# Softmax denominators by 32x32 turns on VectorE instead of products with ones, in a block of attention, MLP and Fourier layer

## The chip, the cores and the metric

The kernel runs on one core of one Trainium2 chip. The metric is the device time in microseconds, the median of several runs. The engines are TensorE (PE; PEld is its weight load), VectorE (DVE), ScalarE (ACT), GpSimd (POOL) and SyncE (SP), which issues nearly all DMAs.

## The reference, cut to what matters

Two layers work on a 48x48 image with 768 channels: 2304 tokens. The first is a transformer block: layer norm, attention with 12 heads of 64 channels and relative positions, projection, MLP. The second filters in the Fourier domain. The change lies in the attention's softmax and what follows it:

```python
attn = jnp.einsum('bqc,bkc->bqk', q * scale, k)
rel_h = jnp.einsum('bhwc,hkc->bhwk', r_q, Rh)
rel_w = jnp.einsum('bhwc,wkc->bhwk', r_q, Rw)
attn = (attn.reshape(B * nh, H, W, H, W) + rel_h[:, :, :, :, None] + rel_w[:, :, :, None, :]).reshape(B * nh, H * W, H * W)
attn = jax.nn.softmax(attn, axis=-1)
out = jnp.einsum('bqk,bkc->bqc', attn, v)
...
out = out @ proj_w + proj_b
x = shortcut + out
```

## The kernel before, in words

All arithmetic is in f32. The kernel has stages: queries, keys and values (to 434 us in the profile), attention (434 to 1452), projection, MLP, Fourier layer.

Attention goes over six pairs of heads (`pr`, 0 to 5; the two heads of a pair are `j` = 0, 1, on 64 partitions each) and, within a pair, over six chunks of `G` = 384 queries (`c`, 0 to 5): 36 chunks. For one chunk the keys are gone through in 18 tiles of 128 (`kt`). For each, `scores` makes transposed scores, keys on partitions and queries along the row, by `content` (L560) and `position` (L569), and ScalarE takes the exponential of both heads at once (L579) into `exps`. No maximum is subtracted. VectorE adds the exponentials up over key tiles: `pairs` (L665) takes two tiles at a time, eight additions in a chunk, the first of them when four tiles are there; `acc` (L669) is their sum, 128 partitions by 2 heads by 384 queries. What is still to be added is the sum over the partitions.

Then come the products with the values, `products` (L592), in six pieces of three key tiles. `between` returns what is put ahead of which piece (a table `work` by piece, 0 to 5): the denominators ahead of piece 5; in chunks 0 to 2 a `relative` for the chunk three further on ahead of piece 0; in chunks 3 and 4 the `columns` of the next pair ahead of pieces 0 to 2, and in chunk 4 a `relative` ahead of piece 3; in chunk 5 two `relative`; none of these in the last pair for chunks 3 to 5. A `relative` makes small products (L292) into the one `small` bank of PSUM, which ScalarE copies twice and VectorE subtracts (L238, `row_lo` and `col_parts`), and issues 24 transfers from SyncE into `terms`. `fetch` and `fetch_values` load the next pair's queries, keys and values from DRAM.

`denominators` (L603) multiplies `acc` by ones, so that every one of 64 rows has the sum of its head; ScalarE copies that to `rden` (L608) and accumulates `sums`. After the products, `finish` copies `op` out of PSUM (L617), adds the value bias times the denominator (L618), inverts the denominator on VectorE (L621), multiplies (L623, which also reorders the queries from blocks to rows), adds the inverse to `inverse` on GpSimd (L624), and stores to `oT` in DRAM (L625). `sums` and `inverse` are later tested for overflow; the test decides by a branch whether a slower general path runs.

Next, the projection reads `oT` by token tile (`og`, L692), and `residual` loads `x` (L685).

The order of PE and SyncE in attention is the order of the program (`manual_schedule`), and so is ScalarE's in the loop over the chunks. VectorE and GpSimd are ordered by a planner, as are instructions outside those scopes.

Of the kernel before, what the change touches and what calls it, by code (L numbers as in the profile page):

```python
# [19 lines left out]
P = 128  # L20
# [26 lines left out]
def block_then_afno(  # L47
# [53 lines left out]
    k_d = [dram.tile([P, T], F32, name=f"k_d{i}") for i in range(NC)]  # L101
    v_d = dram.tile([T, C], F32, name="v_d")
    oT = dram.tile([C, T], F32, name="oT")

    big1 = ctx.enter_context(tc.tile_pool(name="big1", bufs=1))
    main = big1.tile([P, NT * C], F32, name="main")
# [84 lines left out]

    with ExitStack() as flag_scope:
        flag_pool = flag_scope.enter_context(tc.tile_pool(name="flag", bufs=1))
        sums = flag_pool.tile([P, NC * (T // G)], F32, name="sums")
        inverse = flag_pool.tile([P, G], F32, name="inverse")
        nc.vector.memset(inverse, 0.0)


# [5 lines left out]
        with ExitStack() as att:  # L204
# [338 lines left out]
            with tc.manual_schedule(engines={mybir.EngineType.PE, mybir.EngineType.SP}):  # L543
                with ExitStack() as qkv:
                    queries_keys_values(qkv)

                psum = att.enter_context(tc.tile_pool(name="ps_att", bufs=1, space=PSUM))
                small_banks(psum, 1)
                kv_b = att.enter_context(tc.tile_pool(name="att_kv_b", bufs=1))
                o_pool = att.enter_context(tc.tile_pool(name="att_o", bufs=2))  # L550

                by_column = o_pool.tile([P, HW, HW], F32, name="by_column", bufs=1)
                kv = [None, kv_b]
                exps = main.rearrange("p (n j q) -> p n j q", n=NT, j=2)

                def content(pr, c, kt, sp, first):
                    qT, kT = heads[pr][:2]
                    for j in range(2):
                        at = slice(64 * j, 64 * j + 64)
                        nc.tensor.matmul(  # L560
                            sp[:, j, :G], kT[at, ts(kt, P)], qT[at, ts(c, G)],
                            start=first, stop=not first,
                        )

                def position(pr, c, kt, sp, first):
                    a, b = divmod(kt, 3)
                    for j in range(2):
                        at = slice(64 * j, 64 * j + 64)
                        nc.tensor.matmul(  # L569
                            sp[:, j, :G], select[at, a % 2], ready[pr, c][at, a // 2, b],  # L570
                            start=first, stop=not first,
                        )

                def scores(pr, c, kt, p):

                    sp = psum.tile([P, 2, 512], F32, name="sp", bufs=3)
                    for n, part in enumerate((content, position)):
                        part(pr, c, kt, sp, n == 0)
                    nc.scalar.activation(p, sp[:, :, :G], AF.Exp, scale=HD**-0.5)  # L579

                def in_columns(pr, i):

                    q = heads[pr][0].rearrange("p (c b h w) -> p b w c h", c=6, b=3, h=8)
                    nc.scalar.copy(
                        by_column[:, ts(i, 8)].rearrange("p w (c h) -> p w c h", c=6),
                        q[:, i // 2, ds(8 * (i % 2), 8)],
                    )

                def products(op, v, kts):
                    for kt in kts:  # L590
                        for j in range(2):
                            nc.tensor.matmul(  # L592
                                op[ts(j, 64)], v[:, kt, ts(j, 64)], exps[:, kt, j, :],
                                start=(kt == 0), stop=(kt == NT - 1),
                            )

                made = {}

                def denominators(pr, c, acc):

                    den = small_bank()
                    for j in range(2):
                        nc.tensor.matmul(  # L603
                            den[ts(j, 64)], ones[:, 0:64], acc[:, j, :], start=True, stop=True
                        )
                    at = pr * (T // G) + c
                    rden = o_pool.tile([P, G], F32, name="rden", bufs=1)
                    nc.scalar.activation(  # L608
                        rden, den, AF.Identity, accum_out=sums[:, at : at + 1]
                    )  # L610
                    made[pr, c] = rden

                def finish(pr, c, op):

                    rden = made.pop((pr, c))
                    ot = o_pool.tile([P, G], F32, name="ot")
                    nc.scalar.copy(ot, op)  # L617
                    nc.vector.scalar_tensor_tensor(  # L618
                        ot, rden, col(V_VB + pr), ot, ALU.mult, ALU.add
                    )  # L620
                    nc.vector.reciprocal(rden, rden)  # L621
                    o = o_pool.tile([P, G], F32, name="o")
                    nc.vector.tensor_tensor(by_rows(o), by_blocks(ot), by_blocks(rden), ALU.mult)  # L623
                    nc.gpsimd.tensor_tensor(inverse, inverse, rden, ALU.add)  # L624
                    nc.sync.dma_start(out=oT[ts(pr, P), ts(c, G)], in_=o)  # L625

                def between(pr, c, acc):

                    last = pr == NC - 1
                    work = {5: [partial(denominators, pr, c, acc)]}  # L630
                    if c < 3:
                        work[0] = [partial(relative, pr, c + 3)]
                    elif not last and c < 5:
                        for n in range(3):
                            work[n] = [partial(columns, pr + 1, 3 * (c - 3) + n)]
                        if c == 4:
                            work[3] = [partial(relative, pr + 1, 0)]
                    elif not last:
                        work[0] = [partial(relative, pr + 1, 1)]
                        work[2] = [partial(relative, pr + 1, 2)]  # L640
                    if not last and c in (2, 3):
                        for n in range(3):
                            i = 3 * (c - 2) + n
                            work.setdefault(n + (1, 3)[c - 2], []).append(
                                partial(in_columns, pr + 1, i)
                            )
                    return work

                with tc.manual_schedule(engines={mybir.EngineType.Activation}):
                    for pr in range(NC):  # L650
                        for c in range(T // G):
                            if c == 1 and pr < NC - 1:
                                fetch(pr + 1, kv[(pr + 1) % 2])
                            if c == 2 and pr < NC - 1:
                                fetch_values(pr + 1)
                            if c == 4 and pr == NC - 1:
                                nc.sync.dma_start(
                                    out=pw, in_=proj_w.rearrange("(c p) f -> p c f", p=P)
                                )
                            pairs = o_pool.tile([P, 2, 2, G], F32, name="pairs", bufs=1)  # L660
                            for kt in range(NT):
                                scores(pr, c, kt, exps[:, kt])
                                if kt > 2 and kt % 2:
                                    so_far = exps[:, ds(0, 2)] if kt == 3 else pairs
                                    nc.vector.tensor_tensor(  # L665
                                        pairs, so_far, exps[:, ds(kt - 1, 2)], ALU.add
                                    )
                            acc = o_pool.tile([P, 2, G], F32, name="acc")
                            nc.vector.tensor_tensor(acc, pairs[:, 0], pairs[:, 1], ALU.add)  # L669
                            op = psum.tile([P, G], F32, name="op")  # L670
                            work = between(pr, c, acc)
                            for i in range(6):
                                for what in work.get(i, ()):
                                    what()
                                products(op, heads[pr][2], range(3 * i, 3 * i + 3))
                            finish(pr, c, op)

        ln2 = flag_scope.enter_context(tc.tile_pool(name="ln2", bufs=4))
        for i in range(4):
# [847 lines left out]
```

## Time and profile before

| | |
|---|---|
| time, median of 3 runs | 2884.89 us (2884.84 to 2886.05) |
| profiled execution | 2886.02 us, span 2884.2 us |
| PE busy in the span | 2835.7 us (98%) |
| DVE / ACT / POOL busy in the span | 1759.2 / 937.1 / 618.4 us |
| attention, 434 to 1452 us: PE busy | 1017.42 of 1018 us |
| granted TensorE clock, mean | 0.996 |
| L603 in the trace | 144 records of 486 ns (4 in a chunk) |

A row of the timeline gives start and length in microseconds, engine, line, operation, what is written and read, the shape and the number of instructions merged. A bracket at the end gives the idle time before it and what ended it. Consecutive TensorE records overlap, so that the distance from start to start, and not the length of one, is what a product takes of the stage.

### The profile page before, as it was taken

How to read it: one execution, taken by the hardware profiler on the slowest of the kernel's cores; microseconds unless marked ns; L12 is line 12 of the kernel's file. 1: busy time of each engine (PE TensorE's matmuls, PEld its weight loads, DVE VectorE, ACT ScalarE, POOL GpSimd, SP SyncE). 2: the span in 40 equal slices, each digit the busy share in tenths (PEclk: the TensorE clock that was granted, in tenths of full speed). 3: DMA queues.
4: the chain of work that ended last, by engine and by line, in shares of the span. 5: the costliest groups of instructions: out<-in, count | busy, mean ns of one | idle time of the engine just before them, and what ended most of it. 6: DMA issues, size and time to landing. Idle time of an engine off the chain costs nothing. (4 is left out here: it accounts for less than half of the span.)

```text
span 2884.2 us, 41229 instructions
## 1 busy us (share of the span) xinstructions
PE 2835.7 (98%) x15949; PEld 1727.6 (60%) x15949; DVE 1759.2 (61%) x2412; ACT 937.1 (32%) x1538; POOL 618.4 (21%) x589
## 2 busy tenths in 40 slices
PE   8999999999999999999999999999999999999998
PEld 5555655656565555565555555555555555556887
DVE  5343236767676767676723666675666666666665
ACT  1011125757566666565600211122111211112332
POOL 2303010000000000000043322333322322322433
PEclk9999999999999999999999999999999999999999
DMA  4323276262552626445242111212111211113254
GB/s 150 134 96 107 100 163 126 41 129 59 90 122 48 140 37 124 82 68 89 62 165 77 50 56 54 66 59 75 64 66 45 98 55 56 54 56 115 64 157 143
DMA packets 216572, 255.59 MB, mean 89 GB/s; under 512 B 22220, under 2 KB 197036, under 8 KB 214832
## 3 DMA queue, kind: packets, MB, share of 16 engines
q1 hardware_dynamic: 213928, 251.03, 34.1%
q8 instruction: 128, 2.10, 0.3%
q10 hardware_dynamic: 2440, 1.84, 0.2%
q14 instruction: 76, 0.62, 0.1%
HBM read 136.88 MB, written 52.20 MB: 66 GB/s over the span
## 5 line engine op out<-in xcount | busy, mean ns | idle before, releaser
L579 ACT ACTIVATE main<-sp 128x768 f32<-128x768 f32 x648 | 516.7, 812 | 34.1 <-PE sp L569 19.5
L665 DVE TENSOR_TENSOR pairs<-pairs,main 128x1536 f32<-128x1536 f32 x252 | 443.0, 1758 | 27.1 <-DVE pairs L665 0.9
L569 PE MATMUL sp<-terms,select 64*128 64x384 f32 x1296 | 413.4, 630 | 0.0
L1060 DVE TENSOR_TENSOR main<-o,main 128x384 f32<-128x384 f32 x540 | 299.0, 556 | 40.6 <-PE o L1058 2.1
L998 PE MATMUL h<-shared,w 128*128 128x384 f32 x864 | 296.7, 486 | 0.8 <-issue 0.8
L560 PE MATMUL sp<-shared 64*128 64x384 f32 x1296 | 266.9, 488 | 2.2 <-DVE o L460 2.2
L560 PE MATMUL sp<-qT,kT 64*128 64x384 f32 x1296 | 264.1, 484 | 0.0
L624 POOL TENSOR_TENSOR inverse<-inverse,rden 128x384 f32<-128x384 f32 x36 | 49.0, 1360 | 977.3 <-DVE rden L621 977.3
L449 PE MATMUL m<-main 128*128 128x384 f32 x756 | 246.4, 488 | 3.0 <-DVE main L176 2.4
L998 PEld LDWEIGHTS h<-shared,w 128*128 128x128 f32 x864 | 164.1, 190 | 116.6 <-issue 3.2
L998 PE MATMUL h<-shared,w1s 128*128 128x384 f32 x648 | 226.6, 486 | 0.0
L592 PE MATMUL op<-main,shared 128*64 128x384 f32 x1296 | 218.7, 487 | 0.0
L1004 ACT ACTIVATE hT<-c,vec 128x384 f32<-128x384 f32 x108 | 66.4, 615 | 465.9 <-DVE c L1010 465.8
L592 PE MATMUL op<-main,v 128*64 128x384 f32 x1296 | 217.7, 487 | 0.0
L449 PEld LDWEIGHTS m<-main 128*128 128x128 f32 x756 | 143.0, 190 | 104.0 <-issue 4.6
L1010 DVE TENSOR_TENSOR c<-h,u 128x384 f32<-128x384 f32 x108 | 60.1, 557 | 212.4 <-PE h L998 212.4
L1058 PE MATMUL o<-w,hT 128*128 128x384 f32 x432 | 175.4, 488 | 3.3 <-DVE mv L122 2.0
L1058 PE MATMUL o<-w2s,hs 128*128 128x384 f32 x432 | 175.0, 487 | 2.3 <-DVE hs L159 2.3
L569 PEld LDWEIGHTS sp<-terms,select 64*128 64x128 f32 x1296 | 126.0, 187 | 83.7 <-issue 0.5
L998 PEld LDWEIGHTS h<-shared,w1s 128*128 128x128 f32 x648 | 123.1, 190 | 85.9
L618 DVE SCALAR_TENSOR_TENSOR ot<-rden,vec,ot 128x384 f32<-128x384 f32 x36 | 23.5, 654 | 241.0 <-ACT ot L617 241.0
L158 POOL TENSOR_TENSOR w1s<-w 128x384 f32<-128x384 f32 x36 | 36.7, 1020 | 604.7 <-PE o L1058 335.9
(161 smaller groups left out, 4079.0 us busy)
## 6 DMA issues: line engine op xcount, KB each, us to landing
w<-in_mlp_w_dram SPq DMA_DIRECT2D x72, 768.0 KB
terms<-col_parts SPq DMA_DIRECT2D x432, 72.0 KB
terms<-row_hi SPq DMA_DIRECT2D x216, 72.0 KB
terms<-row_lo SPq DMA_DIRECT2D x216, 72.0 KB
main<-in_qkv_w_dram SPq DMA_DIRECT2D x36, 384.0 KB
z<-zt SPq DMA_DIRECT2D x48, 192.0 KB
x<-in_x_blocks_dram SPq DMA_DIRECT2D x18, 384.0 KB
k_d<-o SPq DMA_DIRECT2D x36, 192.0 KB
```

Of the source, the lines that this page charges most:

```text
L449: nc.tensor.matmul(bank, a[:, c, :], b[:, c, :], start=(first and c == 0), stop=(c == 2), skip_group_check=not first,)
L560: nc.tensor.matmul(sp[:, j, :G], kT[at, ts(kt, P)], qT[at, ts(c, G)], start=first, stop=not first,)
L569: nc.tensor.matmul(sp[:, j, :G], select[at, a % 2], ready[pr, c][at, a // 2, b], start=first, stop=not first,)
L579: nc.scalar.activation(p, sp[:, :, :G], AF.Exp, scale=HD**-0.5)
L592: nc.tensor.matmul(op[ts(j, 64)], v[:, kt, ts(j, 64)], exps[:, kt, j, :], start=(kt == 0), stop=(kt == NT - 1),)
L624: nc.gpsimd.tensor_tensor(inverse, inverse, rden, ALU.add)
L665: nc.vector.tensor_tensor(pairs, so_far, exps[:, ds(kt - 1, 2)], ALU.add)
L998: nc.tensor.matmul(bank[i], a[:, c, :], b[:, c, :], start=(start and c == 0), stop=(c == 2), skip_group_check=not start,)
L1004: nc.scalar.activation(h[:, i, ts(k, G)], src, AF.Gelu, bias=col(V_B1 + 2 * n + i))
L1010: nc.vector.tensor_tensor(t, src, other, ALU.add)
L1058: nc.tensor.matmul(bank[k], a, b, start=start, stop=True, skip_group_check=not start)
L1060: nc.vector.tensor_tensor(dst, bank[k], dst, ALU.add)
```

## The change

The sum over partitions is made in another way. VectorE turns `acc` in blocks of 32x32 (`turned`), which puts 32 keys of a block along the row, and sums each 32 (`part`, 24 sums on each partition). One product of `part` with `gather` (a 128x32 matrix with a one where the partition is equal to the column modulo 32) adds the four groups of partitions; its result is 24 x 32, the 768 denominators of two heads by 384 queries, each once. `denominators` stands ahead of piece 1 and the product, in `inverses`, ahead of piece 4. VectorE inverts 24x32 values and adds to `sums`, and GpSimd adds to `inverse`.

To multiply the results, the inverses must stand on all 64 rows of their head. They are written to DRAM (`den_d`, `left_apart`) and read back with a broadcast (`spread_out`, two transfers), both from SyncE ahead of piece 5. A chunk's inverses are read back one chunk later than they are written, and used in `scaled` another chunk later. In the last pair from chunk 3 on they are read at once. `scaled` multiplies by `spread` on VectorE, and GpSimd then adds the value bias; `stored` stores the result a chunk later (in the last pair, from chunk 3 on, also at once). `finish` keeps only the copy out of PSUM. VectorE's order in the loop becomes that of the program, and `fetch_values` is called in chunk 3 in place of 2.

```diff
-        sums = flag_pool.tile([P, NC * (T // G)], F32, name="sums")
-        inverse = flag_pool.tile([P, G], F32, name="inverse")
+        sums = flag_pool.tile([P, 32], F32, name="sums")
+        inverse = flag_pool.tile([P, 32], F32, name="inverse")
...
+                ND = 2 * G // 32
+                gather = o_pool.tile([P, 32], F32, name="gather", bufs=1)
+                nc.vector.tensor_reduce(
+                    gather, ident.rearrange("p (g a) -> p a g", a=32), AX.X, ALU.add
+                )
+                parts = [o_pool.tile([P, 48], F32, name=f"part{i}", bufs=1) for i in range(2)]
...
                 def denominators(pr, c, acc):
 
+                    at = pr * (T // G) + c
+                    turned = o_pool.tile([P, 2 * G], F32, name="turned", bufs=1)
+                    nc.vector.transpose(turned, acc.rearrange("p j q -> p (j q)"))
+                    part = parts[at % 2]
+                    nc.vector.tensor_reduce(
+                        part[:, :ND], turned.rearrange("p (b i) -> p b i", i=32), AX.X, ALU.add
+                    )
+
+                def inverses(pr, c):
+
+                    at = pr * (T // G) + c
+                    part = parts[at % 2]
                     den = small_bank()
-                    for j in range(2):
-                        nc.tensor.matmul(
-                            den[ts(j, 64)], ones[:, 0:64], acc[:, j, :], start=True, stop=True
-                    at = pr * (T // G) + c
-                    rden = o_pool.tile([P, G], F32, name="rden", bufs=1)
-                    nc.scalar.activation(
-                        rden, den, AF.Identity, accum_out=sums[:, at : at + 1]
-                    )
+                    nc.tensor.matmul(den[:48, :32], part, gather, start=True, stop=True)
+                    rden = o_pool.tile([ND, 32], F32, name="rden")
+                    nc.vector.reciprocal(rden, den[:ND, :32])
+                    nc.vector.tensor_tensor(sums[:ND], sums[:ND], den[:ND, :32], ALU.add)
+                    nc.gpsimd.tensor_tensor(inverse[:ND], inverse[:ND], rden, ALU.add)
...
                 def finish(pr, c, op):
 
-                    rden = made.pop((pr, c))
-                    ot = o_pool.tile([P, G], F32, name="ot")
+                    ot = o_pool.tile([P, G], F32, name="ot", bufs=3)
                     nc.scalar.copy(ot, op)
-                    nc.vector.scalar_tensor_tensor(
-                        ot, rden, col(V_VB + pr), ot, ALU.mult, ALU.add
-                    )
-                    nc.vector.reciprocal(rden, rden)
-                    o = o_pool.tile([P, G], F32, name="o")
-                    nc.vector.tensor_tensor(by_rows(o), by_blocks(ot), by_blocks(rden), ALU.mult)
-                    nc.gpsimd.tensor_tensor(inverse, inverse, rden, ALU.add)
-                    nc.sync.dma_start(out=oT[ts(pr, P), ts(c, G)], in_=o)
+                    made[pr, c].append(ot)
+
+                def left_apart(pr, c):
+
+                    (rden,) = made[pr, c]
+                    nc.sync.dma_start(
+                        out=den_d[pr * (T // G) + c].rearrange("(n i) -> n i", i=32), in_=rden
+                    )
...
+                def spread_out(keep):
+
+                    while len(to_spread) > keep:
+                        pr, c = to_spread.pop(0)
+                        at = pr * (T // G) + c
+                        spread = o_pool.tile([P, G], F32, name="spread")
+                        for j in range(2):
+                            nc.sync.dma_start(
+                                out=spread[ts(j, 64)],
+                                in_=den_d[at, ts(j, G)].partition_broadcast(64),
+                            )
+                        to_scale.append((pr, c, spread))
+
+                def scaled(keep):
+
+                    while len(to_scale) > keep:
...
+                        nc.vector.tensor_tensor(
+                            by_rows(o), by_blocks(ot), by_blocks(spread), ALU.mult
                         )
+                        nc.gpsimd.tensor_scalar(o, o, col(V_VB + pr), None, ALU.add)
+                        results.append((pr, c, o))
...
                 def between(pr, c, acc):
 
                     last = pr == NC - 1
-                    work = {5: [partial(denominators, pr, c, acc)]}
+                    work = {
+                        1: [partial(denominators, pr, c, acc)],
+                        4: [partial(inverses, pr, c)],
+                        5: [partial(left_apart, pr, c), stored],
+                    }
+                    if last and c > 2:
+                        work[5] += [partial(spread_out, 0), partial(scaled, 1), stored]
+                    else:
+                        work[5] += [partial(spread_out, 1), partial(scaled, 1)]
...
-                with tc.manual_schedule(engines={mybir.EngineType.Activation}):
+                with tc.manual_schedule(
+                    engines={mybir.EngineType.Activation, mybir.EngineType.DVE}
+                ):
...
-                            if c == 2 and pr < NC - 1:
+                            if c == 3 and pr < NC - 1:
                                 fetch_values(pr + 1)
...
+                    scaled(0)
+                    stored()
```

More of the change, by code (lines that the diff above doesn't have):

```diff
@@ L103, in block_then_afno @@
     oT = dram.tile([C, T], F32, name="oT")
+    den_d = dram.tile([NC * (T // G), 2 * G], F32, name="den_d")
     big1 = ctx.enter_context(tc.tile_pool(name="big1", bufs=1))
@@ L193, in block_then_afno @@
         flag_pool = flag_scope.enter_context(tc.tile_pool(name="flag", bufs=1))
-        sums = flag_pool.tile([P, NC * (T // G)], F32, name="sums")
-        inverse = flag_pool.tile([P, G], F32, name="inverse")
+        sums = flag_pool.tile([P, 32], F32, name="sums")
+        inverse = flag_pool.tile([P, 32], F32, name="inverse")
+        nc.vector.memset(sums, 0.0)
         nc.vector.memset(inverse, 0.0)
@@ L595, in products @@
                             )
-                made = {}
-                def denominators(pr, c, acc):
-                    den = small_bank()
-                    for j in range(2):
-                        nc.tensor.matmul(
-                            den[ts(j, 64)], ones[:, 0:64], acc[:, j, :], start=True, stop=True
-                        )
-                    at = pr * (T // G) + c
-                    rden = o_pool.tile([P, G], F32, name="rden", bufs=1)
-                    nc.scalar.activation(
-                        rden, den, AF.Identity, accum_out=sums[:, at : at + 1]
-                    )
-                    made[pr, c] = rden
@@ L613, in finish @@
-                def finish(pr, c, op):
-                    rden = made.pop((pr, c))
-                    ot = o_pool.tile([P, G], F32, name="ot")
-                    nc.scalar.copy(ot, op)
-                    nc.vector.scalar_tensor_tensor(
-                        ot, rden, col(V_VB + pr), ot, ALU.mult, ALU.add
-                    )
-                    nc.vector.reciprocal(rden, rden)
-                    o = o_pool.tile([P, G], F32, name="o")
-                    nc.vector.tensor_tensor(by_rows(o), by_blocks(ot), by_blocks(rden), ALU.mult)
-                    nc.gpsimd.tensor_tensor(inverse, inverse, rden, ALU.add)
-                    nc.sync.dma_start(out=oT[ts(pr, P), ts(c, G)], in_=o)
+                ND = 2 * G // 32
@@ new lines, in block_then_afno @@
+                gather = o_pool.tile([P, 32], F32, name="gather", bufs=1)
[3 more added lines that the diff above has]
+                parts = [o_pool.tile([P, 48], F32, name=f"part{i}", bufs=1) for i in range(2)]
+                for part in parts:
+                    nc.vector.memset(part, 0.0)
+                def denominators(pr, c, acc):
+                    at = pr * (T // G) + c
[5 more added lines that the diff above has]
+                    )
@@ new lines, in inverses @@
+                def inverses(pr, c):
+                    at = pr * (T // G) + c
+                    part = parts[at % 2]
+                    den = small_bank()
+                    nc.tensor.matmul(den[:48, :32], part, gather, start=True, stop=True)
[3 more added lines that the diff above has]
+                    nc.gpsimd.tensor_tensor(inverse[:ND], inverse[:ND], rden, ALU.add)
+                    made[pr, c] = [rden]
@@ new lines, in block_then_afno, with finish @@
+                made, to_spread, to_scale, results = {}, [], [], []
+                def finish(pr, c, op):
+                    ot = o_pool.tile([P, G], F32, name="ot", bufs=3)
+                    nc.scalar.copy(ot, op)
+                    made[pr, c].append(ot)
[4 more added lines that the diff above has]
+                    )
+                    made[pr, c] = []
+                    to_spread.append((pr, c))
@@ new lines, in scaled @@
+                def scaled(keep):
+                    while len(to_scale) > keep:
+                        pr, c, spread = to_scale.pop(0)
+                        (ot,) = made.pop((pr, c))
+                        o = o_pool.tile([P, G], F32, name="o")
+                        nc.vector.tensor_tensor(
+                            by_rows(o), by_blocks(ot), by_blocks(spread), ALU.mult
+                        )
+                        nc.gpsimd.tensor_scalar(o, o, col(V_VB + pr), None, ALU.add)
+                        results.append((pr, c, o))
@@ L627, in between, with stored @@
+                def stored():
+                    while results:
+                        pr, c, o = results.pop(0)
+                        nc.sync.dma_start(out=oT[ts(pr, P), ts(c, G)], in_=o)
                 def between(pr, c, acc):
                     last = pr == NC - 1
-                    work = {5: [partial(denominators, pr, c, acc)]}
+                    work = {
[7 more added lines that the diff above has]
+                        work[5] += [partial(spread_out, 1), partial(scaled, 1)]
@@ L634, in between @@
                         for n in range(3):
-                            work[n] = [partial(columns, pr + 1, 3 * (c - 3) + n)]
+                            work.setdefault(n, []).append(partial(columns, pr + 1, 3 * (c - 3) + n))
                         if c == 4:
```

## The prediction

> **What bounds the kernel now.** I read the busy line of the page first, then the attention stage alone (the windows view), then one chunk in order of time, and last the rows of the lines that the change touches.
>
> ```profile
> PE 2835.7 (98%) x15949; PEld 1727.6 (60%) x15949; DVE 1759.2 (61%) x2412; ACT 937.1 (32%) x1538; POOL 618.4 (21%) x589
> ```
> ```profile
> 434.00:1452.00 1018.00, 1017.42 (x8537) 591.95 (x8536) 727.00 (x489) 627.96 (x895) 51.61 (x38) 1.00 0.46 90
> ```
>
> The second line has the window, its length, then busy time of PE, PEld, DVE, ACT and POOL, the granted clock, the DMA share and GB/s. In these 1018 us, which hold nearly all 36 chunks, PE is busy for 1017.42; VectorE has 291 us to spare, ScalarE 390, GpSimd nearly everything. So the stage ends when TensorE has done its instructions, and time is gained only by giving TensorE less or lost by making it wait. A busy PE may still be one whose records overlap, so the price of a product is read from starts, here one chunk's end on PE:
>
> ```profile
> 1008.79 0.93 PE L292 MATMUL small<-qT,relT 128*48 128x48 f32 x32
> 1009.55 9.86 PE L592 MATMUL op<-main,v 128*64 128x384 f32 x60
> 1019.24 0.81 PE L603 MATMUL small<-acc,ones 128*64 128x384 f32 x4
> 1019.88 2.10 PE L592 MATMUL op<-main,v 128*64 128x384 f32 x12
> 1021.92 0.92 PE L560 MATMUL sp<-qT,kT 64*128 64x384 f32 x4
> ```
>
> Column one is the start. The denominators (L603) start at 1019.24 and the next product at 1019.88: 0.64 us for four records, 0.16 each, though the source view gives 486 ns as the length of one (they overlap). A chunk with one `relative` takes 28.09 us (1021.91 less 993.82, the chunk starts).
>
> VectorE in the same chunk:
>
> ```profile
> 1013.96 0.96 DVE L669 TENSOR_TENSOR acc<-pairs 128x768 f32<-128x768 f32 x1
> 1014.83 0.55 DVE L238 TENSOR_TENSOR row_lo<-shared,row_hi 128x384 fp32r<-128x384 f32 x1
> 1022.55 0.62 DVE L618 SCALAR_TENSOR_TENSOR ot<-rden,vec,ot 128x384 f32<-128x384 f32 x1 [7.16 <-ACT ot L617]
> 1023.27 2.55 DVE L621 RECIPROCAL rden<-rden 128x384 f32<-128x384 f32 x1
> 1025.86 0.56 DVE L623 TENSOR_TENSOR o<-ot,rden 128x384 f32<-128x384 f32 x1
> 1026.41 2.48 DVE L665 TENSOR_TENSOR pairs<-main 128x1536 f32<-128x1536 f32 x1
> ```
>
> `acc` is ready at 1014.92, four microseconds ahead of its product: VectorE is off the path, by a margin that the change eats into.
>
> **What the Trainium skill says.** "VectorE: DVE Perf Modes", The three transpose paths: VectorE turns only 32x32 blocks, 128x128 bf16 in 311 ns. No turn is in this trace. The same page, Rules for kernel authors, says that a reduction runs at one element per cycle at best; the trace agrees: L719 with 36 elements took 191 ns, L720 with 384 took 553, 1.04 ns an element. "GPSIMD Engine Reference", Specifications: GpSimd shares SBUF interfaces with VectorE operations that have two SBUF inputs. The trace agrees: the first `pairs` addition takes 2.48 us beside GpSimd's `inverse` addition (1025.90 to 1027.27), and 1.76 in the first chunk, where GpSimd is idle. "DMA: Bandwidth & Descriptors", Anatomy of one DMA: some 2.0 us fixed for a transfer; the trace gives no landing times here, so I use it for the round trip through DRAM.
>
> **The change, part by part.** The sum is made against the profiled execution, 2886.02 us (span 2884.2), 1.1 over the median 2884.89; I take the difference off the median.
>
> 1. *Removed on TensorE*: 36 x 0.64 = **23.1 us**, all on the path.
> 2. *Added on TensorE*: one product of 48 columns of weights against 32 columns in two records (f32 gives two per product, as L603's four for two show). Nearest row: L292, 32 records of 48 columns from 1008.79 to 1009.55, 0.024 each, including the change to L592's shape. Two make 0.05; a 64-column weight load afterwards (137 ns) has no long product to hide under, so up to 0.2. I take 0.1: 36 x 0.1 = **3.6 us**. Bounds 1.8 and 7.2. Net 19.5.
> 3. *Turn and row sum on VectorE*, and its order fixed as written. The product now stands at piece 4, three k-tiles earlier: 12 records, 1.92 us. Its first weight load would come at 1018.92 (L603's) - 1.92 = 1017.00, or 3.04 us after `acc` starts. The first `pairs` addition loses its GpSimd neighbour and 0.72 us; the other seven follow at 1.85 us apiece (12.93 for seven), VectorE's own pace, so `acc` starts 0.72 earlier against the chunk: the limit is 3.76. It can't start earlier still, because the first addition already began at 1026.41, just when the fourth exponential was done (1023.07 + 4 x 0.82). From `acc`'s start: 0.87 to `row_lo`, 0.47 until the turn starts (the two follow at that distance elsewhere), turn 0.96, 0.09 between dependent operations, sum 0.95 (553 + 384 x 1.04). Sum **3.34**, 0.42 early. Cost zero, hidden under 12 products; without that cover it would be 1.9 us a chunk.
>  The turn is the unknown. Lower bound 0.96, one element per cycle as `acc` (128x768 in 958 ns). Upper: the skill's 311 ns scaled by six, an estimate of 1.87. I take 0.96, since 311 ns less the 0.16 fixed cost of these rows (958 - 768 x 1.04) leaves 1.2 ns an element, near the lower one. At 1.87 the product waits 0.5 us in the 18 chunks with c < 3, about 0.9 in the last pair's c = 3 to 5 (no `relative` ahead of the products there: `acc` to weight load is 2.33 + 0.72 = 3.05 against 3.05 used, no slack even now) and little elsewhere, since `columns` and a second `relative` add 0.76 us of PE each: 9 + 3 = 12 us. With the low value I charge 0.5 us for those last three.
> 4. *VectorE's other work*: gone are 0.62 + 2.55; new are a reciprocal of 32 (6.2 ns each by L621, some 0.35 us), an addition of 32 (0.19) and the moved product (0.56). With turn and sum the engine's 19.95 us in a chunk of 28.1 falls below 19. The small ones run from piece 4 on and end about 2 us before the chunk does; the next addition is due 4.5 us into the next chunk. Zero; VectorE isn't short of time.
> 5. *The new waits*. VectorE waits for `spread` ahead of the product `scaled`, with the next chunk's `pairs` behind it. `spread` was asked for one chunk before. SP is the queue that could make it late: each `relative` issues 24 transfers at 0.64 us, 15.4 us; from c = 4 to c = 0 of the next pair it issues without a pause. The change adds three transfers a chunk (one store, two reads), 2 us. There the reads of the fourth chunk leave some 25 us into chunk 0, just as VectorE wants them; with 2 to 4 us to land it idles until 28 or 29, and has until 28 + 4.5. Zero, with about 4 us of margin, five times in the kernel. `terms` are made two chunks ahead elsewhere; for c = 0 they are asked for a chunk ahead, before the new transfers. The moved `fetch_values` (1.15 MB) has over two chunks left. GpSimd's `inverse` addition shrinks and an addition of 128x384 (1.0 us) joins: idle otherwise.
> 6. *ScalarE* loses 0.49 + 0.19 us per chunk in a stretch in which it waits: zero.
> 7. *The end*. The last chunk's result goes through DRAM: two transfers of 2.0 us after the reciprocal, then 0.56 and 1.0. The reciprocal comes some 3 us before the products end, so the store leaves about 3 us after their end; before, it left at 1456.23, 6.3 after (1447.81 + 2.10). Loads for the projection (og, at 1437.5) stood ahead of that store; if they fall behind it TensorE waits up to 5 us, otherwise it neither gains nor loses. I take zero.
>
> Sum: -23.1 + 3.6 + 0.5 = **-19.0 us: 2886.0 becomes 2867.0, and the median 2866**. A measurement of this kernel can tell about 0.2% (5.8 us) from no change.
>
> **The rivals.**
> - *Part of the gain is waited away* (turn near 1.87 us, or the small product 0.2 us and the end 5 us): 12 us or 9 us back, 2874 to 2879. For it: the slack of 0.42 us is small, semaphores take part of it. Against: the skill's figure without its fixed cost. Chance 0.24.
> - *The small product waits for VectorE in nearly every chunk* and the kernel gets slower. Place: the weight load of `part` at piece 4, with six k-tiles of `products`, and then the next scores, behind it on PE. At 3.2 ns an element the turn takes 2.5 us: late by 1.1 in 18 chunks, 0.6 in five c = 5 chunks, 1.6 in three, 28 us, against 19.5 saved: 2893. It decides from a turn of about 2.1 us, where the waits eat the saving, and measures as slower from about 2.4. A `spread` that comes later than the 4 us of margin would add to it. Against: nothing on VectorE here but the reciprocal costs over 1.05 ns an element. Chance 0.13.
> - *Balanced*, between these: 2879.1 to 2890.7. Chance 0.07.
> - *The removed products were not on the path*, ScalarE being the bound with 18 x 0.82 us of exponentials: then no change. Against: it idles in the product pieces, and PE starts its first three score groups of a chunk, with free buffers, at the same 0.82 us. It is in the balanced case.
>
> **How the numbers follow.** The likeliest is the sum, 2866, chance 0.56. Faster: 0.56 + 0.24 = 0.80; within 0.2%: 0.07; slower: 0.13. The low end is the whole 23.1 saved with the small products nearly free, 2862 less a microsecond of noise; the high end takes in the partial rival and part of the balanced case: 2861 to 2882.
>
> **What would show it.** The `small` product with `part` and `gather` at about 0.1 us from start to next start, in place of 0.64; c = 1 chunks of 27.5 us in place of 28.09; the first `pairs` addition at 1.76 us; the turn as a row of about 0.96 us. Wrong would be: PEld waiting for the row sum in the list of waits, VectorE's `o` waiting for `spread` by more than 6 us, or a gap on PE between attention and projection.

## The result, and the profile after

| | before | after |
|---|---|---|
| time, median | 2885.47 us (2884.84 to 2887.24) | 2862.11 us (2861.51 to 2863.60) |
| profiled execution, its span | 2886.02, 2884.2 us | 2862.67, 2860.6 us |
| first score product to first projection product | 1033.3 us | 1013.5 us |

The ratio is 0.9919 (95% interval 0.9902 to 0.9936): faster by 23 us, 19 to 28. The first view is the page's busy line and the windows view of attention after (window, length, then busy PE, PEld, DVE, ACT, POOL, clock, DMA share, GB/s):

```profile
PE 2811.8 (98%) x15877; PEld 1733.5 (61%) x15877; DVE 1695.7 (59%) x2488; ACT 916.4 (32%) x1466; POOL 625.5 (22%) x625
```
```profile
434.00:1430.00 996.00, 995.42 (x8429) 596.15 (x8425) 666.69 (x564) 606.21 (x822) 58.70 (x71) 1.00 0.52 98
```

PE is as full as before, over a shorter stage: it still sets the end, and has less to do. The end of one chunk on PE, in order of time:

```profile
969.47 0.92 PE L294 MATMUL small<-qT,relT 128*48 128x48 f32 x32
970.23 7.93 PE L594 MATMUL op<-main,v 128*64 128x384 f32 x48
977.98 0.19 PE L623 MATMUL small<-gather,part 128*48 128x32 f32 x1
977.99 0.54 PE L594 MATMUL op<-main,v 128*64 128x384 f32 x1
978.01 0.21 PE L623 MATMUL small<-gather,part 128*48 128x32 f32 x1
978.06 4.06 PE L594 MATMUL op<-main,v 128*64 128x384 f32 x23
982.05 0.92 PE L562 MATMUL sp<-qT,kT 64*128 64x384 f32 x4
```

Products and small product together go from 970.23 to 982.05, 11.82 us; before, from 1009.55 to 1021.92, 12.37. The difference, 0.55, is what each chunk became shorter by: all 35 distances between one chunk's end and the next are 0.54 to 0.56 us less. VectorE in another chunk of the same kind:

```profile
986.54 1.76 DVE L725 TENSOR_TENSOR pairs<-main 128x1536 f32<-128x1536 f32 x1 [7.38 <-ACT main L581]
988.41 12.93 DVE L725 TENSOR_TENSOR pairs<-pairs,main 128x1536 f32<-128x1536 f32 x7
1001.37 0.96 DVE L729 TENSOR_TENSOR acc<-pairs 128x768 f32<-128x768 f32 x1
1002.25 0.55 DVE L240 TENSOR_TENSOR row_lo<-shared,row_hi 128x384 fp32r<-128x384 f32 x1
1002.72 0.97 DVE L612 STREAM_TRANSPOSE turned<-acc 128x768 f32<-128x768 f32 x1
1003.72 0.95 DVE L614 TENSOR_REDUCE part<-turned 128x24 f32<-128x768 f32 x1
1005.85 0.34 DVE L625 RECIPROCAL rden<-small 24x32 f32<-24x32 f32 x1 [1.17 <-PE small L623]
1006.12 0.12 DVE L626 TENSOR_TENSOR sums<-sums,small 24x32 f32<-24x32 f32 x1
1006.17 0.53 DVE L666 TENSOR_TENSOR o<-ot,spread 128x384 f32<-128x384 f32 x1
```

The turn takes 0.97 us. The row sum is there at 1004.67, and the small product's weight load starts 0.53 us later (the same in nearly every chunk with c < 3; 1.3 to 2.5 us with c = 3 to 5; 0.06 to 0.14 in the last three chunks). The bracket in the first row says that VectorE had stood idle for 7.38 us before this chunk's exponentials let it start: it is still off the path.

The stage is 19.8 us shorter, the medians differ by 23.4. The rest lies outside attention, where nothing was changed (us, one profiled execution each; e1 to e8 are the experiments below, e2 is code of before with one product cut):

| | up to the first score | projection | MLP | Fourier | sum |
|---|---|---|---|---|---|
| before | 417.2 | 151.4 | 1025.7 | 252.7 | 1847.0 |
| after | 416.4 | 150.0 | 1024.3 | 252.6 | 1843.4 |
| e2 | 416.8 | 151.3 | 1025.4 | 250.7 | 1844.2 |
| e6 | 416.7 | 150.3 | 1024.0 | 251.0 | 1842.0 |
| e8 | 418.7 | 151.2 | 1024.2 | 251.4 | 1845.5 |

In the traces of the ten kernels the sum goes from 1842.0 to 1847.0; the trace of before is the highest, and e2, with the same code outside attention, is 2.7 us below it. The kernel before itself took from 2878.72 to 2886.64 us in 23 runs on one chip. Most of the difference is granted clock, as the windows view shows in the projection, the first row before and the second after (the clock is the third number from the end):

```profile
1522.90:1529.70 6.80, 5.19 (x8) 2.83 (x9) 4.24 (x13) 0.88 (x3) 0.32 (x1) 0.50 0.59 188
1503.30:1506.70 3.40, 3.01 (x5) 1.82 (x6) 3.06 (x9) 0.59 (x2) 0.00 (x0) 0.50 0.52 148
```

TensorE ran at half clock for 6.8 us there before and for 3.4 us after. Over all ten traces, the seven with 6.8 us at half clock have a projection of 151.2 to 151.6 us, the three with 3.4 us one of 150.0 to 150.3. In the MLP the trace of before has two such stretches of 3.4 us and that of after one. At half clock 3.4 us hold 1.7 us of work, so that by estimate each further stretch costs up to 1.7 us; the two stages differ by 1.4 each. So 19.8 us belong to the change, and the other 3.6 to the executions that were traced.

### The profile page after: what moved, and what is told of

The parts are those of the page before. It is cut to its first block, busy times and chain, and to the rows that moved or that the text cites. A ratio compares the mean times of both kernels' runs of the same rounds, so it can differ in the third digit from the quotient of the medians.

```text
span 2860.6 us, 41333 instructions
## 1 busy us (share of the span) xinstructions
PE 2811.8 (98%) x15877; PEld 1733.5 (61%) x15877; DVE 1695.7 (59%) x2488; ACT 916.4 (32%) x1466; POOL 625.5 (22%) x625
## 5 line engine op out<-in xcount | busy, mean ns | idle before, releaser
L627 POOL TENSOR_TENSOR inverse<-inverse,rden 24x32 f32<-24x32 f32 x36 | 15.1, 418 | 959.7 <-DVE sums L626 916.2
L725 DVE TENSOR_TENSOR pairs<-main 128x1536 f32<-128x1536 f32 x36 | 63.3, 1759 | 250.6 <-ACT main L581 250.6
```

The lines of the kernel that those rows point to most:

```text
L725: nc.vector.tensor_tensor(pairs, so_far, exps[:, ds(kt - 1, 2)], ALU.add)
```

## Experiments

Ratios are to the kernel before in the same group of runs, with the 95% interval; its median was 2883.94 us in the group of e1 to e4 and 2886.91 in that of e5 to e8. "Attention" is from the first score to the first projection product, 1013.5 us in the changed kernel. All but e2 are edits of the changed kernel. In the traces of e1, e3 and e5 to e8 the first chunk is 0.8 us shorter for a reason that is not their edit: the others have half clock for 3.4 us at its start.

**e1: the products with ones put back.**

```diff
+                def with_ones(acc):
+                    den = small_bank()
+                    for j in range(2):
+                        nc.tensor.matmul(
+                            den[ts(j, 64)], ones[:, 0:64], acc[:, j, :], start=True, stop=True
+                        )
...
-                        5: [partial(left_apart, pr, c), stored],
+                        5: [partial(with_ones, acc), partial(left_apart, pr, c), stored],
```

> The changed kernel with the two products of acc with ones put back ahead of piece 5, their result unused: everything of the change stays but the removal on TensorE. If TensorE's time is the whole of the gain, it gives back 36 x 0.64 = 23 us and ends at 2885, within 2 us of the kernel before; each chunk longer by 0.64 us. If VectorE's shorter work or its fixed order brought part of the gain (rival), it stays below the kernel before by that part: at 2880 or less if that is 5 us. The stages before and after attention tell whether the 3.5 us that the two traces differ by outside of attention belong to the change (they stay at -0.8 and -2.7) or to the execution (they don't).

Measured: 2886.21 us, ratio 1.0010 (1.0003 to 1.0017); attention 1035.9, each chunk but the first 0.64 us longer than after and 0.09 longer than before. Everything else of the change together brings nothing. The 0.09 is the whole price of the small product, bare of what it replaces. Outside attention the differences that the expectation asks about come out at -0.4 and -2.9 us against the trace before, so they stayed; but e2, which has the code of before there, has -0.3 and -2.4. They belong to the trace of before and not to the change. The medians agree: over 20 and 23 runs they differ by 2.3 us, attention alone by 2.5.

**e2: the kernel before, with less product.**

```diff
-                            den[ts(j, 64)], ones[:, 0:64], acc[:, j, :], start=True, stop=True
+                            den[ts(j, 64), :32], ones[:, 0:64], acc[:, j, :32],
+                            start=True, stop=True,
...
-                    nc.vector.memset(bank, 0.0)
+                    nc.vector.memset(bank, 1.0)
```

> The kernel before with its products with ones cut to 32 of 384 columns, the rest of the denominators left out (what stands in the bank is taken in their place): TensorE's work taken away and nothing else of the change made. If TensorE's time is the whole of the gain: 36 x (0.64 - 0.15) = 18 us faster, 2867 to 2869, with VectorE's reciprocal of 2.55 us, the long first pairs addition of 2.48 us and ScalarE's copy all still there. If VectorE's relief was needed for the gain: 2875 or more.

Measured: 2864.74 us, ratio 0.9936 (0.9919 to 0.9952), 19.2 us less; attention 1014.2, 19.1 less than before. With the long reciprocal, the long first addition and ScalarE's copy all in place, nearly the same gain comes. e1 and e2 settle it from both sides: the gain is TensorE's time and not VectorE's.

**e3: each turn twice.**

```diff
+                    nc.vector.transpose(turned, acc.rearrange("p j q -> p (j q)"))
```

> The changed kernel with every turn done twice: the row sum is ready 1.0 us later. The trace after shows 0.53 us between the row sum's end and the weight load of the small product in the chunks with c < 3, 1.3 to 2.5 with c = 3 to 5, and 0.06 to 0.14 in the last three. If the small product waits on nothing else, PE then waits about 0.5 us (0.6 with the semaphore) in 18 chunks and 1.0 in the last three: 9 + 3 to 11 + 3 us, 2874 to 2876. If VectorE has other room that the trace doesn't show (rival): 2862 to 2866. If VectorE's order behind the turn holds up more than this product: 2880 or more.

Measured: 2870.09 us, ratio 0.9956 (0.9939 to 0.9972), attention 1020.7, 7.2 us more: 0.33 us in chunks with c < 3, none with c = 3 to 5, 0.64 in the last three. The place is as expected and the size is not. A waiting weight load starts 0.12 us after the row sum, so in c < 3 it was 1.01 - (0.53 - 0.12) = 0.60 late, and PE lost only 0.33. The rest is the weight load's lead, shown by the same chunk after (first row; its product starts at 977.98, above) and in e3:

```profile
977.66 0.12 PEld L623 LDWEIGHTS small<-gather,part 128*48 128x48 f32 x1 [0.18 <-issue]
```
```profile
981.91 0.16 PEld L624 LDWEIGHTS small<-gather,part 128*48 128x48 f32 x2 [0.79 <-issue]
981.94 0.20 PE L624 MATMUL small<-gather,part 128*48 128x32 f32 x1
```

After, the weights are loaded 0.32 us ahead of their product, while products of `op` still run; in e3 only 0.03 us ahead. So 0.29 us of lateness is absorbed.

**e4: the small product one piece earlier.**

```diff
-                        4: [partial(inverses, pr, c)],
+                        3: [partial(inverses, pr, c)],
...
-                            work[3] = [partial(relative, pr + 1, 0)]
+                            work[3].append(partial(relative, pr + 1, 0))
```

> The changed kernel with the small product ahead of piece 3 in place of 4 (in chunk 4 ahead of the relative there): 12 records of products, 1.92 us, of its cover are gone. From the margins in the trace after: 1.4 us of wait in 18 chunks, 0.2 in five with c = 3, about 0.2 in five with c = 4 (the relative now stands behind it), 0.6 in five with c = 5, 1.8 in three: 36 us, 2898, slower than the kernel before. If the wait is hidden by PE's own queue, or caught up by the scores (rival): 2862 to 2870.

Measured: 2902.87 us, ratio 1.0066 (1.0049 to 1.0083), attention 1051.9. Chunks lose 1.25 us with c < 3, 0.08 with c = 3, 0.46 with c = 5: each 0.12 to 0.15 less than expected, again by the lead of the weight load (in c < 3 it is 1.92 - 0.53 + 0.12 = 1.51 late, less 0.29). The last three lose 1.6 to 1.9, near the expected 1.8. Only c = 4 is far off, 1.58 against 0.2. The list of waits of e4 (who waited, for whom, us in total, times, longest), and one such chunk on PE:

```profile
PE small L623 <- DVE part L614: 24.4, 25, 1.7
PE small L294 <- DVE sums L626: 7.0, 5, 1.4
```
```profile
558.84 0.25 PE L623 MATMUL small<-gather,part 128*48 128x32 f32 x2
560.48 0.93 PE L294 MATMUL small<-qT,relT 128*48 128x48 f32 x32 [1.39 <-DVE sums L626]
```

The `relative` behind the small product writes the same PSUM bank, the only one of its kind, and waits until VectorE has read the denominators; on VectorE the two `col_parts` subtractions stand ahead of that. So the rival of the prediction that ends slower is a real one: three key tiles of cover, 1.92 us, are the difference between 0.8% faster and 0.7% slower.

**e5: written, read and used in one chunk.**

```diff
-                    if last and c > 2:
-                        work[5] += [partial(spread_out, 0), partial(scaled, 1), stored]
-                    else:
-                        work[5] += [partial(spread_out, 1), partial(scaled, 1)]
+                    work[5] += [partial(spread_out, 0)]
...
                             finish(pr, c, op)
-                    scaled(0)
+                            scaled(0)
```

> The changed kernel with the inverses read back and used in the same chunk: both reads stand behind the write ahead of piece 5, and the multiplication behind the copy of op, in every chunk. Only the distance between write, read and use is taken away. From the trace after: write to use took 7.7 us in the last chunk, where SP was nearly free. Where SP has no transfers of terms in hand (c = 3, and 4 and 5 of the last pair) VectorE gets spread some 3.5 us into the next chunk, in time for the additions due at 4.5: no loss. Where a relative has left 15 us of transfers in SP's queue, spread comes 11 us into the next chunk or later, VectorE stands still with the pairs behind it and the small product comes late by 7 us or more: over 18 chunks and more in the five with two relatives, 120 to 220 us, 2980 to 3080. If the waits on VectorE are absorbed by its 7.4 us of idle time per chunk (rival): 2862 to 2870, and the distance in pieces buys nothing.

Measured: 3181.50 us, ratio 1.1019 (1.1001 to 1.1037), attention 1335.9: worse than the worst expected. Waits of e5, VectorE's and PE's, then SP's queue:

```profile
DVE o L666 <- DMA spread<-den_d: 421.9, 23, 32.2
PE small L623 <- DVE part L614: 261.0, 28, 22.3
```
```profile
SPq L307 <- DVE row_lo L240: 217.6, 23, 15.4
SPq L641 <- DVE sums L626: 162.7, 8, 25.0
SPq L654 <- DMA den_d<-rden: 49.5, 36, 2.9
```

The waits close a loop: SP's transfers of `terms` from `row_lo` wait for VectorE, which stands still for `spread`, which SP issues only behind those `terms`. In one chunk, `row_lo` is made at 705.74, SP issues `terms` from 706.32 until the write of the inverses at 717.84 and the reads at 720.50, `o` starts at 724.00, the additions follow, and the next `row_lo` comes at 740.37: 34.6 us a turn, against 27.5 for PE's work. A chunk pays for the `relative` of the chunk before it. The 18 chunks behind one ahead of piece 0 lose 7.3 us on average, as expected. The five behind the one in c = 4, which stands ahead of piece 3, lose 14 to 16 us and were not counted, and the five behind two lose 24. Nor was the clock counted. A stretch of the same chunk behind its wait, in the windows view:

```profile
708.30:713.40 5.10, 5.09 (x18) 2.85 (x20) 0.39 (x2) 0.00 (x0) 0.24 (x1) 0.50 0.77 116
```

Around each of PE's 27 waits of 3.5 us and more, half the clock was granted, from 2.2 to 5.4 us into the wait to 2.8 to 5.9 us behind its end. PE waited for 262 us in all, and for 116 us more it worked at half clock, which by estimate costs 58: together 320 of the 322 us that were lost. A distance of one chunk opens the loop, as e8 shows, and is needed.

**e6: VectorE's order left to the planner.**

```diff
-                    engines={mybir.EngineType.Activation, mybir.EngineType.DVE}
+                    engines={mybir.EngineType.Activation}
```

> The changed kernel with VectorE's order left to the planner, as it was before, ScalarE's fixed. If the order as written is only a means of keeping the turn right behind acc and row_lo, and the planner puts them there too: 2862 within 2 us. If the planner puts the multiplication of an earlier chunk or other work ahead of the turn, or waits in another order, the small product is late by 0.5 us or more per chunk beyond its margin: 2870 or more (rival).

Measured: 2863.57 us, ratio 0.9924 (0.9907 to 0.9940), attention 1013.8. The planner sets the turn ahead of `row_lo`, and from the second pair on the margin with c < 3 is 0.87 us in place of 0.53. The chunks are as long as after but for the last, which is 1.1 us longer: the planner sets one `o`, which waits for `spread`, among its additions. That is all that the order written out brings.

**e7: GpSimd busy beside the first addition.**

```diff
+                    beside = o_pool.tile([P, G], F32, name="beside", bufs=1)
+                    for _ in range(6):
+                        nc.gpsimd.tensor_tensor(beside, ot, ot, ALU.add)
```

> The changed kernel with six additions of 128x384 with two inputs added on GpSimd at each chunk's start (their result unused), so that GpSimd works while VectorE makes the chunk's first pairs addition. If GpSimd's work beside it is what made that addition 2.48 us before and 1.76 after: it is again near 2.5 us or more here, the row sum comes at least 0.7 us later, and with a margin of 0.53 us, of which the weight load's lead gives 0.3 more, the small product is late by 0.1 us in 18 chunks and by 0.4 in three: 2 to 5 us, 2864 to 2867. If the length came from something else that the change removed (the operations before it on VectorE): 1.76 us still and 2862.

Measured: 2876.21 us, ratio 0.9964 (0.9952 to 0.9975), attention 1024.6. VectorE and GpSimd in one chunk of e7:

```profile
993.73 2.36 DVE L728 TENSOR_TENSOR pairs<-main 128x1536 f32<-128x1536 f32 x1 [7.38 <-ACT main L581]
996.19 13.57 DVE L728 TENSOR_TENSOR pairs<-pairs,main 128x1536 f32<-128x1536 f32 x7
```
```profile
990.03 6.75 POOL L639 TENSOR_TENSOR beside<-ot 128x384 f32<-128x384 f32 x6 [3.56 <-ACT ot L635]
996.75 2.74 POOL L672 TENSOR_SCALAR o<-o,vec 128x384 f32<-128x384 f32 x1
```

The first addition is long again, 2.36 us, beside GpSimd's additions. Its length does not follow the time spent side by side: here that is all of the addition, in the kernel before only the 0.86 us from 1026.41 to 1027.27, and it grew there by 0.72. The expectation counted only that one; the seven that follow took 13.57 in place of 12.93, beside GpSimd's one-input addition of the value bias, which was pushed there, and with c < 3 the row sum came 1.0 to 1.2 us late and not 0.7. With the 0.12 us of a waiting load, and less the margin of 0.53 and the lead of 0.29, that makes the 0.30 us (c = 0) and 0.54 (c = 1 and 2) that most of these chunks lost.

**e8: read back at once, used one chunk later.**

```diff
-                    if last and c > 2:
-                        work[5] += [partial(spread_out, 0), partial(scaled, 1), stored]
-                    else:
-                        work[5] += [partial(spread_out, 1), partial(scaled, 1)]
+                    work[5] += [partial(spread_out, 0), partial(scaled, 1)]
+                    if last and c > 2:
+                        work[5] += [stored]
```

> The changed kernel with the inverses read back in the chunk that wrote them in all chunks, and used one chunk later in place of two. SP now waits for the write to land, 3 to 4 us a chunk, ahead of the reads. If SP's room between two chunks' terms is enough (it issued without a pause from c = 4 to c = 0 of the next pair only, 60 us of 167): 2862 within 2 us, and VectorE's waits for spread at the pairs' borders (10 us in all, not paid by TensorE) shrink. If SP's waits push terms past the start of their chunk (rival), TensorE waits for terms at each pair's first chunks: 2870 or more.

Measured: 2864.16 us, ratio 0.9925 (0.9908 to 0.9942), attention 1012.7. SP waited 50 us in all for the writes, and nothing came late by it: behind the first, every chunk is as long as after, within 0.01 us. But VectorE's waits for `spread` did not shrink: 21.0 us in six, the one after the last chunk included, against 16.6 in seven after. One chunk of distance is enough, two buy nothing more. No version here beats the changed kernel by more than the spread of runs.

## Why the prediction was right

- *What bounds, and the removal (step 1).* Right: 0.64 us a chunk, by e1 and by the trace (36 of them are 23.0, not 23.1).
- *The small product (step 2).* Taken at 0.1, measured 0.64 - 0.55 = 0.09.
- *The chain to the row sum (step 3).* The turn was the unknown, between 0.96 and 1.87; it took 0.97, as quick as the addition of the same size. The low value was a bet that came true: against the slower rival the prediction says that nothing but the reciprocal costs over 1.05 ns an element, but in the trace before the subtraction into `col_parts` (L238) took 0.85 us for 384 elements, 2.2 ns each. The first addition lost its GpSimd neighbour and its 0.72 us; e7, with a neighbour put back, has it long again. Margin forecast 0.42, measured 0.53. The 0.5 us charged to the last three chunks was not paid: they became 0.54 to 0.56 us shorter like all others, since the weight load's lead, which the sum did not have, covers it.
- *VectorE's small work and ScalarE (steps 4 and 6).* Zero, by e2 and e1.
- *The waits for* `spread` *(step 5).* After, the list of waits has them inside attention:

```profile
DVE o L666 <- DMA spread<-den_d: 10.1, 6, 3.7
PEld small L623 <- DVE part L614: 0.8, 3, 0.4
```

 Five of the six are the ones foreseen, in chunk 0 of the next pair: 0.8 to 1.6 us each, ended by 26 us into the chunk, some 2.9 us after the second read was issued. The longest, 3.7, stands in the last pair, where the inverses are read at once. TensorE does not pay for any. The second row is a sign that was named for being wrong: the weight load did wait for the row sum, in the last three chunks, within its lead.
- *The end (step 7).* Mis-sized, at no cost. SP's queue after the last chunk:

```profile
1417.52 1.55 SPq L754 DMA_DIRECT2D og<-oT  x3
...
1425.85 0.32 SPq L641 DMA_DIRECT2D den_d<-rden  x1
1426.27 0.34 SPq L747 DMA_DIRECT2D main<-in_x_dram  x1
1426.66 0.42 SPq L754 DMA_DIRECT2D og<-oT  x1
1430.07 1.09 SPq L654 DMA_DIRECT2D spread<-den_d  x2
...
1438.16 0.32 SPq L675 DMA_DIRECT2D oT<-o  x1
```

 Write to use took 7.7 us (`o` started at 1433.55) where two transfers of 2.0 us had been counted (the page that the prediction names gives this figure for transfers that GpSimd issues; these are SyncE's), and the store left 8.8 us after the products' end in place of 3. `o` waited 6.5 us for `spread`, over the 6 that were to be a sign of being wrong. It cost nothing: the first three `og` loads stood ahead, at 1417.52, and PE's gap before the projection is 0.58 us in both traces.

The sum was 19.0 us for a stage that gave 19.8; the 0.8 are the 0.5 not paid and 0.01 us a chunk on the small product, rounded. The measured 23.4 has 3.6 us that belong to the other stages, mostly to their clock. So 0.8 of the 3.9 us by which 2866 was off come from its own steps, and the rest from what it could not see. Of the rivals, the late small product, the waited-away gain and ScalarE as the bound did not happen, and e4 and e3 show the first two at their price.

## What to carry to other kernels

Where one engine is full, price a change by starts on that engine, and treat the work handed to others as a question of arrival: add up their chain to the instruction that the full engine will wait at, and move that instruction back until there is margin. A value that goes out through a queue and comes back should be used a round of work later when the queue's own transfers wait for the engine that uses it. Before a gain smaller than the spread of the unchanged stages is believed, compare stage by stage, and compare the granted clock too.

## What was not expected of the hardware

- A row sum 0.60 us late cost TensorE 0.33 us: in this stream of 0.16 us records a weight load starts 0.32 us ahead of its product, and that lead took up the rest.
- A product of 32 columns between long ones costs 0.09 us for two records; their weight loads hide nearly wholly.
- GpSimd's addition with one tensor input, too, ran beside slower VectorE additions in e7 (2.74 us in place of 1.24 for it, 13.57 in place of 12.93 for them); that this one and no tail of the six before it did it was not separated.
- A write of 3 KB to DRAM and its use by the same queue took 4.2 us from issue to the dependent issue in the last chunk of the changed kernel, with other loads around it, and 1.3 to 2.9 us in all chunks of e8 but the last (3.9).
- In e5 each of TensorE's 27 waits of 3.5 us and more went with half clock, until 2.8 to 5.9 us behind its end. In attention in e4, whose waits were at most 1.7 us long, the clock was full but for 3.4 us in the first chunk.
